# Mixer and FFN in one kernel: segment sums of ten tiles moved beside the FFN, its last products two tiles behind, and the first steps in another order

## The chip, the core and the metric

The kernel runs on one NeuronCore of a Trainium2 chip. The metric is the device time of one execution in microseconds (us). Three runs of the kernel before gave 1754.32 us in the median (1753.77 to 1755.31). Engines are named as in the profile: PE is TensorE (PEld its weight loads), DVE is VectorE, ACT is ScalarE, POOL is GpSimd, SP is SyncE, which issues most of the DMAs.

## What is computed

The input is `hidden_states`, 4 sequences of 256 tokens and 512 features, so 1024 tokens (T). It is normalised once (`xn`) and goes into two branches; the result is `x + s * g`.

```python
zxbcdt = xn @ in_proj_w.T            # gate 8192 | x 8192, B 1024, C 1024 | dt 128
xBC = silu(causal_conv4(xBC) + conv_b)
dt  = softplus(dt + dt_bias); Adt = -exp(A_log) * dt
L   = exp(segment_sum(Adt))          # decay from token j to token i, 0 for j > i
y   = ((C B^T) * L) @ (x * dt) + D * x         # per head; 128 heads of 64, 8 groups
s   = rmsnorm_per_group(y * silu(gate)) * norm_w @ out_proj_w.T
g   = silu((silu(xn @ gate_w.T) * (xn @ up_w.T)) @ down_w.T)   # FFN, 1792 wide, ternary weights
```

The reference works in chunks of 32 tokens; the kernel works with blocks of 128, two for each sequence, which gives the same sums. `segment_sum` of a row of `Adt` is, in the kernel, one scan along the free axis of a tile of 128 x 1024: `state = (state + m) * after`, where `after` is 1 above the diagonal of each block and 0 elsewhere. The row of a head is the same on all 128 partitions.

## The kernel before

**Two parts.** The first, `front` (from the start to 310.2 us in the profile), runs the normalisation, the FFN and, woven into it, `dt`, and for each of the 8 groups the tiles of B and C and their block products ("scores"). The second is a loop of 64 steps (L767), one for each tile of 128 channels of `x` (two heads) and of the gate.

**front.** The FFN has two halves of the tokens by 14 tiles of 128 of its width, so 28 tiles in sequence (L534). A tile makes `pg` and `pu` (16 products into two PSUM banks, L285), `sg = silu(pg) * pu` (ACT L539, DVE L548), splits it into a high and a low part `hh` (ACT L563) and `hl` (DVE L565), and adds 8 products of the tile before to four accumulators `pf` (`down`, L293). So the last products of a tile are made one tile behind. POOL casts the ternary weights (L225). `ffn_out` (L297) scales the finished accumulators, takes their SiLU and stores them.

Three times in each tile `next(pieces)` (L540, L551, L564) runs one turn of `all_pieces` (L481), so there are 84 turns. `bc_pieces(g)` (L413) begins at turn 11 + 8g and takes 14 turns: the products of B and C for a group, four sums of weights on DVE for the next group (`combine_to`), four additions (L434, L437, L440), three convolution taps for each of B and C (L181), two SiLUs and the score blocks (L460, L463). From turn 20 on `early_pieces` (L469) takes five turns for each of the 11 tiles 1 to 11: it loads the weights of that tile into `wq`, makes their four sums with `combine_to` into `sq`, and stores them in the DRAM tensor `early`.

**The sums of weights.** The products of a step are made with seven block products in place of eight (Strassen's form, in Winograd's variant), so each pair of weight tiles needs four sums or differences of 128 x 256 (L142 to L146).

**A step i.** On PE: seven products of two matmuls each (L173: `px`, `pq`, `px`, `pz`, `px`, `px`, `pq`) for gate and `x` of tile i; between them the transposes of tile i-1 (L625); then 48 small products `py` of tile i-1 (L666: for each sequence those with `v0`, then `v1`, then `v0t`). From step 10 on, 24 or 32 products `po` of the output projection of the group before come in between (L722). On ACT: copies of PSUM halves, the convolution's SiLU (L186), the exponentials of the scanned tiles `m` (L615), `y_begin` (L652), squares for the norm (L861, L864), the scaling of `wo` by the norm's weights (L856), the last tap (L177), the gate's SiLU (L899, L903). On DVE, steps 1 to 8: scan of `m` (L612), gating of tile i-2 (L673), second scan, `m * gm` and `mo * gm` for two heads (L618, L619), `xpad` add (L873), `v0`, `v0t` (L633), `v1` (L642), `gT` add (L889), three taps (L181). Up to LEAD = 9 the convolution's SiLU and both exponentials of a tile are issued in the step after it, later in its own step.

**Order.** Each engine works through its own list in the order in which the program issues instructions (`manual_schedule`); waits are made by semaphores. SP's list holds the DMAs of both parts in that order. `m` has five buffers, `mo` four, `w` two, `sq`/`sqacc` one.

For tiles up to EARLY = 11 the step loads the weights and their sums (L801 to L803, L918) in place of making them; from step 11 on `combine_w` makes them on DVE. The sums of the output weights of a group (`right_factors`, L708: four differences of 128 x 1024) are made at wn = 7 (two), on = 0 and on = 1, for the first group in steps 9, 9, 10 and 11. `wn`, `on` count the steps of a group from step 2.

Of the kernel before, what the change touches and what calls it, by code (L numbers as in the profile page):

```python
# [74 lines left out]
LEAD = 9  # L75
EARLY = 11
# [5 lines left out]
def mixer_ffn(ctx: ExitStack, tc: tile.TileContext, x, in_w, conv_w, conv_b, dt_bias, a_log, d_col,  # L82
# [44 lines left out]
    early = dram.tile([EARLY, P, 4, KT // 2, P], F32, name="early")  # L127
# [59 lines left out]


    def front(pre, one_of, fp, f2, hp, wq):
# [31 lines left out]
        def cast_ffn(n):  # L221
            ws = []
            for tag, wi in loads.pop(n):
                w = fp.tile([P, HID], F32R, name=tag, tag=tag)
                nc.gpsimd.tensor_copy(w, wi)  # L225
                ws.append(w)
            return ws
# [241 lines left out]
        def early_pieces():  # L469
            for n in range(EARLY):  # L470
                w = wq.tile([P, 2, KT, P], F32, name="wq")
                for m, i in enumerate((n + 1, CT + n + 1)):
                    nc.sync.dma_start(w[:, m], in_w[i])
                for _ in range(2):
                    yield
                s = wq.tile([P, 4, KT // 2, P], F32, name="sq")
                yield from combine_to(s[:, 0], s[:, 1], s[:, 2], s[:, 3], w)
                nc.sync.dma_start(early[n], s)
                yield

        def all_pieces():  # L481

            turn, chains = 0, [first_pieces()]
            later = []
            while chains or later or turn < 11 + 8 * G:
                if turn == 6:
                    later.append(dt_pieces())
                if turn >= 11 and (turn - 11) % 8 == 0 and (turn - 11) // 8 < G:
                    chains.insert(0, bc_pieces((turn - 11) // 8))
                if turn == 20:  # L490
                    later.append(early_pieces())
# [41 lines left out]
        last = None  # L533
        for n, (h, f) in enumerate(steps):  # L534
            if n + 2 < len(steps):
                load_ffn(n + 2)
            pg = project_exact(ws[0], xh, xl)
            sg = fp.tile([P, HALF], F32, name="sg")
            nc.scalar.activation(sg, pg, AF.Silu, scale=gs[:, f:f + 1])  # L539
            next(pieces, None)  # L540
            if f == 1 and h:
                ffn_out(h - 1, done, (1, 2))
# [9 lines left out]
            if f == 1 and h:  # L552
                ffn_out(h - 1, done, (3,))
            if last:
                down(*last)
                if f == 0:
                    done = last[0]
            if f == 0:
                pfs = [p.tile([P, HID], F32, name="pf", tag=tag)
                       for p, tag in ((ps_o, "o"), (ps_o, "o"), (ps_y, "y"), (ps_y, "y"))]  # L560
            hh = fp.tile([P, HALF], F32R, name="hh")
            hl = fp.tile([P, HALF], F32R, name="hl")
            nc.scalar.copy(hh, sg)  # L563
            next(pieces, None)  # L564
            nc.vector.tensor_tensor(hl, sg, hh.bitcast(F32), ALU.subtract)  # L565
            if f == 0 and h:
                ffn_out(h - 1, done, (0,))
            last = pfs, f, hh, hl, wd
        down(*last)
# [3 lines left out]
        return held["a"]  # L573

    with (tc.manual_schedule(), tc.tile_pool(name="pre", bufs=NT) as pre,
          tc.tile_pool(name="one_of", bufs=1) as one_of, tc.tile_pool(name="fp", bufs=3) as fp,
          tc.tile_pool(name="f2", bufs=2) as f2, tc.tile_pool(name="hp", bufs=1) as hp,
          tc.tile_pool(name="wq", bufs=1) as wq):
        a = front(pre, one_of, fp, f2, hp, wq)
# [15 lines left out]
    def load_rows(ct):  # L595
        ms = []
        for h in range(2):
            m = mp.tile([P, T], F32, name="m")
            nc.sync.dma_start(m, rows[2 * ct + h, 0:T].partition_broadcast(P))
            ms.append(m)  # L600
        return ms
# [8 lines left out]

    def decay_scan(m):
        nc.vector.tensor_tensor_scan(m, m, after, 0.0, ALU.add, ALU.mult)  # L612
# [43 lines left out]
    def y_products(ps, vs, ms, offs):  # L656
# [4 lines left out]
        for b in range(NB):  # L661
            py = ps[b // 2][:, b % 2, :]
            for q, v, stop in ((0, v0, True), (1, v1, False), (1, v0t, True)):
                for h, d in enumerate(halves):
                    m = off[h][:, b, :] if v is v0t else diag[h][:, b, q, :]
                    nc.tensor.matmul(py[d, q * P:(q + 1) * P], v[:, b, h, :], m,  # L666
                                     start=False, stop=stop, skip_group_check=True)
# [9 lines left out]
    def come(g, k):  # L677

        return k // 2 if g == G - 1 else max(k // 2, k - 2)
# [82 lines left out]
    with tc.manual_schedule():  # L762
# [3 lines left out]
        sqacc = rs = ya = outs = left = nxt = ob = sa = sb = sc = None  # L766
        for i in range(CT):  # L767
# [31 lines left out]
            if i + 1 <= EARLY:  # L799
                w = wp.tile([P, 2, KT, P], F32, name="w")  # L800
                nc.sync.dma_start(w[:, 0], in_w[i + 1])  # L801
                nc.sync.dma_start(w[:, 1, 0:2], early[i, :, 3])
                nc.sync.dma_start(w[:, 1, 2:4], in_w[CT + i + 1, :, 2:4])  # L803
            elif i + 1 < CT:
                w = load_w(i + 1, CT + i + 1)
# [22 lines left out]
            if here:  # L828
                product(pq, s1, t1, True)
                product(px, s2, t2, False)  # L830
                nc.scalar.copy(gT[:, HALF:], px)  # L831
                if lead:
                    decay_exp(ms[i - 1][1])
                if i:
                    decay_scan(ms[i][0])

                product(pz, a12, x21, False, (0,))
            if old:
# [5 lines left out]
                yps[i - 1] = y_begin(i - 1, xTs[i - 1])  # L844
            if here:
# [4 lines left out]
                nc.scalar.copy(xpad_h[1], by_batch(px))  # L850
            if og >= 0 and on == 0:
                sd = norm_sums(sqacc)
# [4 lines left out]
            if older:  # L857
                yf = yg.rearrange("p b l -> p (b l)")
                if (i - 2) % PER_G == 0:
                    sqacc = sqp.tile([P, T], F32, name="sqacc")  # L860
                    nc.scalar.activation(sqacc, yf, AF.Square)  # L861
                else:
                    sq = sqp.tile([P, T], F32, name="sq")
                    nc.scalar.activation(sq, yf, AF.Square)  # L864
# [4 lines left out]
            if i < CT + 1 and wg >= 0 and wn == PER_G - 1:  # L869
                rights[wg], toms[wg] = right_factors(wos[wg])  # L870
                toms[wg].pop(0)()
# [4 lines left out]
            for n, turn in ((wg, PER_G - 1), (og, 0), (og, 1)):  # L876
                if i < CT + 1 and n >= 0 and on == turn:
                    toms[n].pop(0)()
            if here:
                product(px, a22, t4, False)  # L880
                nc.scalar.copy(xpad_h[0], by_batch(px))
                if i == 0:
                    decay_scan(ms[i][0])
                    decay_scan(ms[i][1])
                product(pq, s4, x22, False)
            if old and og < 0:
                vs.append(values_1(i - 1, xTs[i - 1]))
# [5 lines left out]
            if old and og >= 0:  # L893
                vs.append(values_1(i - 1, xTs[i - 1]))
            if here:
# [8 lines left out]
            if old:  # L904
                y_products(yps[i - 1], vs, ms.pop(i - 1), offs.pop(i - 1))
# [5 lines left out]
            if here:  # L911
                conv_taps(i, xTs[i], xpad)
# [3 lines left out]
                if i + 1 <= EARLY:  # L916
                    s = scp.tile([P, 3, KT // 2, P], F32, name="s")
                    nc.sync.dma_start(s, early[i, :, 0:3])  # L918
                    a = factors(w, s)
# [4 lines left out]
                if i:  # L924
# [46 lines left out]
        y_products(py, vs, ms.pop(last), offs.pop(last))  # L971
# [110 lines left out]
```

## Time and profile before

| what | value |
|---|---|
| median of three runs | 1754.32 us |
| the profiled execution itself | 1755.07 us |
| its span, first to last instruction | 1753.4 us, so 1.7 us lie around it |
| PE busy | 1723.2 us (98%) |
| DVE busy | 1449.3 us (83%) |
| ACT busy | 1068.0 us (61%) |
| DMA | 342.16 MB, mean 195 GB/s |
| mean granted TensorE clock | 0.999 |

A line of the page's fifth part gives a group of instructions: line, engine, operation, output and inputs by name, shapes, count, then the busy time in us, the mean in ns of one, and the idle time of its engine just before it with what ended most of it. The view by windows gives the busy time of each engine in stretches of the span. The chain of waits follows the execution back from its last instruction, at each step to what released it. Busy PE is not PE at its peak, since ends of matmuls are modelled.

### The profile page before, as it was taken

How to read it: one execution, taken by the hardware profiler on the slowest of the kernel's cores; microseconds unless marked ns; L12 is line 12 of the kernel's file. 1: busy time of each engine (PE TensorE's matmuls, PEld its weight loads, DVE VectorE, ACT ScalarE, POOL GpSimd, SP SyncE). 2: the span in 40 equal slices, each digit the busy share in tenths (PEclk: the TensorE clock that was granted, in tenths of full speed). 3: DMA queues.
4: the chain of work that ended last, by engine and by line, in shares of the span. 5: the costliest groups of instructions: out<-in, count | busy, mean ns of one | idle time of the engine just before them, and what ended most of it. 6: DMA issues, size and time to landing. Idle time of an engine off the chain costs nothing.

```text
span 1753.4 us, 22592 instructions
## 1 busy us (share of the span) xinstructions
PE 1723.2 (98%) x8494; PEld 1106.2 (63%) x8494; DVE 1449.3 (83%) x1742; ACT 1068.0 (61%) x1418; POOL 196.8 (11%) x238
## 2 busy tenths in 40 slices
PE   9999999999999999999999999999999999999999
PEld 6566667445456666666666666666666666666677
DVE  5757666699988898889888888888888888888876
ACT  4544333577766666666666667666666666666640
POOL 3221121000000000111011101110111011101110
PEclk9999999999999999999999999999999999999999
DMA  6254553567767666776677667776777577757785
GB/s 228 79 185 154 213 180 109 188 217 227 214 205 208 201 199 193 210 202 185 199 213 200 193 185 214 199 206 179 214 199 216 166 214 201 215 165 214 212 231 172
DMA packets 164091, 342.16 MB, mean 195 GB/s; under 512 B 15376, under 2 KB 55952, under 8 KB 163984
## 3 DMA queue, kind: packets, MB, share of 16 engines
q1 hardware_dynamic: 141296, 287.78, 47.5%
q0 software_dynamic: 22688, 52.96, 17.0%
q8 instruction: 67, 1.10, 0.2%
q14 instruction: 40, 0.33, 0.1%
HBM read 236.08 MB, written 76.28 MB: 178 GB/s over the span
## 4 chain that ended last, share of the span: by engine, by line
PE 86%; DVE 10%; ACT 2%; issue 2%; DMA 1%; SPq 0%; ACTq 0%; DVEq 0%
PE px L173 24%; PE po L722 22%; PE pq L173 13%; PE py L666 9%; PE pz L173 6%; PE pp L285 4%; PE tp L625 3%; PE pf L293 2%; DVE m L612 2%; DVE xT L181 2%; PE pg L460 1%; DVE cT L181 1%; PE pv L684 1%; DVE m L618 1%; DMA m<-rows 1%
## 5 line engine op out<-in xcount | busy, mean ns | idle before, releaser
L612 DVE TENSOR_TENSOR_SCAN m<-m,after 128x1024 f32<-128x1024 f32 x128 | 292.1, 2283 | 0.4 <-DMA m<-rows 0.4
L173 PE MATMUL px<-xc,w 128*128 128x512 f32 x576 | 274.4, 599 | 6.2 <-ACT xpad L424 2.9
L181 DVE SCALAR_TENSOR_TENSOR xT<-xpad,cw,xT 128x1024 f32<-128x1024 f32 x192 | 246.2, 1282 | 4.6
L722 PE MATMUL po<-wo,ya 128*128 128x256 f32 x768 | 176.5, 379 | 0.0
L666 PE MATMUL py<-m,v 128*64 128x128 f32 x2048 | 160.6, 276 | 3.7 <-DVE v L642 3.7
L618 DVE TENSOR_TENSOR m<-m,gm 128x1024 f32<-128x1024 f32 x128 | 154.9, 1210 | 1.4 <-ACT m L615 1.4
L722 PEld LDWEIGHTS po<-wo,ya 128*128 128x128 f32 x768 | 141.5, 190 | 17.0 <-issue 0.2
L173 PEld LDWEIGHTS px<-xc,w 128*128 128x128 f32 x576 | 99.4, 191 | 81.2 <-issue 69.3
L908 POOL DMA_DIRECT2D sqacc<-sq x54 | 46.1, 853 | 898.5 <-ACT sq L864 852.6
L173 PE MATMUL pz<-xnT,w 128*128 128x512 f32 x288 | 146.1, 593 | 0.0
L173 PE MATMUL px<-xnT,w 128*128 128x512 f32 x288 | 141.9, 615 | 0.0
L173 PE MATMUL px<-xc,s 128*128 128x512 f32 x288 | 135.8, 594 | 4.9 <-ACT pz L821 2.1
L173 PE MATMUL pq<-xnT,s 128*128 128x512 f32 x288 | 136.8, 597 | 2.6 <-DVE xpad L873 1.7
L615 ACT ACTIVATE m<-m 128x1024 f32<-128x1024 f32 x128 | 135.3, 1058 | 0.7
L173 PE MATMUL pq<-xc,s 128*128 128x512 f32 x288 | 135.5, 593 | 0.3 <-DVE gT L889 0.3
L666 PEld LDWEIGHTS py<-m,v 128*64 128x64 f32 x2048 | 116.9, 137 | 25.7 <-issue 19.8
L625 PEld LDWEIGHTS tp<-ident,xT 128*128 128x128 f32 x512 | 67.7, 141 | 100.9 <-issue 86.6
L722 PE MATMUL po<-tw,sy 128*128 128x256 f32 x512 | 115.9, 379 | 0.0
L722 PEld LDWEIGHTS po<-tw,sy 128*128 128x128 f32 x512 | 97.2, 190 | 13.2
L831 ACT COPY gT<-px 128x512 f32<-128x512 f32 x64 | 37.4, 584 | 103.4 <-PE px L173 103.4
L173 PEld LDWEIGHTS px<-xc,s 128*128 128x128 f32 x288 | 54.2, 190 | 72.4 <-issue 65.3
L666 PE MATMUL py<-mo,v 128*64 128x128 f32 x1024 | 99.5, 273 | 0.0
(181 smaller groups left out, 3058.8 us busy)
## 6 DMA issues: line engine op xcount, KB each, us to landing
m<-rows SPq DMA_DIRECT2D x128, 512.0 KB, 6.4
w<-in_in_w SPq DMA_DIRECT2D x133, 256.0 KB, 6.9
mo<-rows SPq DMA_DIRECT2D x128, 256.0 KB, 7.2
gated<-yg SPq DMA_DIRECT2D x64, 512.0 KB, 8.3
ya<-gated SPq DMA_DIRECT2D x30, 1024.0 KB, 7.1
sqacc<-sq POOLq DMA_DIRECT2D x54, 512.0 KB, 5.9
wo<-in_out_w SPq DMA_DIRECT2D x64, 256.0 KB, 7.1
acc<-sa POOLq DMA_DIRECT2D x23, 512.0 KB, 5.8
```

What stands on the lines that cost most here:

```text
L173: nc.tensor.matmul(pp, a[:, k, :], b[:, k, :], start=start and k == 0, stop=k == KT // 2 - 1, skip_group_check=not start)
L181: nc.vector.scalar_tensor_tensor(xT, xpad[:, :, k:k + L], cw[:, i, k:k + 1], xT, ALU.mult, ALU.add)
L285: nc.tensor.matmul(pp, w[:, k * P:(k + 1) * P], part[:, k, :], start=(k == 0 and part is xh), stop=(k == KT - 1 and part is xl))
L293: nc.tensor.matmul(pf, part[:, i * P:(i + 1) * P], wd, start=(f == 0 and part is hh), stop=(f == FT - 1 and part is hl))
L612: nc.vector.tensor_tensor_scan(m, m, after, 0.0, ALU.add, ALU.mult)
L615: nc.scalar.activation(m, m, AF.Exp)
L618: nc.vector.tensor_mul(m, m, gm[:, 0:T])
L625: nc.tensor.transpose(tp[:, b, :], xT[:, b, c * P:(c + 1) * P], ident)
L666: nc.tensor.matmul(py[d, q * P:(q + 1) * P], v[:, b, h, :], m, start=False, stop=stop, skip_group_check=True)
L722: nc.tensor.matmul(po, a[:, k, :], b[:, k, :], start=start and k == 0, stop=k == HG - 1, skip_group_check=not start)
L831: nc.scalar.copy(gT[:, HALF:], px)
L908: nc.gpsimd.dma_start(sqacc, sq, accum_op=ALU.add)
```

## The change

It has these parts:

1. `early_pieces` no longer makes sums of weights. In 20 of the turns 23 to 80 (those with (t - 11) mod 8 of 2, 3 or 5, without 48) it scans the row tile of one of the 20 heads of tiles 0 to 9, and stores the result in `early`, now 20 tensors of 128 x 1024. The rows are loaded up to two ahead into three buffers.
2. The steps 0 to 9 load the scanned tiles (`load_rows` reads `early`) and scan nothing; they make the four sums of weights of the next tile themselves, two ahead of the first tap and two behind the last.
3. The FFN's last products run two tiles behind (`pending`); `wd` has four buffers, `wg` and `wu` two; `ffn_out` of the first half comes some turns later. The weights of tile 1 are loaded at the end of `front`.
4. In steps 0 to 9 (`fill`): the square comes ahead of the copy into `xpad` and `y_begin` behind it; the last tap and the first tap come ahead of `v1`, which comes ahead of the `gT` add; the products with `v1` come last for all sequences.
5. LEAD is 10, EARLY is 10. For the first group the output weights are loaded and scaled two for each step, and the first two differences of `right_factors` are made in steps 7 and 8.

```diff
-LEAD = 9
-EARLY = 11
+LEAD = 10
+EARLY = 10
...
-        def early_pieces():
-            for n in range(EARLY):
-                w = wq.tile([P, 2, KT, P], F32, name="wq")
-                for m, i in enumerate((n + 1, CT + n + 1)):
-                    nc.sync.dma_start(w[:, m], in_w[i])
-                for _ in range(2):
-                    yield
-                s = wq.tile([P, 4, KT // 2, P], F32, name="sq")
-                yield from combine_to(s[:, 0], s[:, 1], s[:, 2], s[:, 3], w)
-                nc.sync.dma_start(early[n], s)
+        def early_pieces(turn):
+            turns = [t for t in range(23, 81) if (t - 11) % 8 in (2, 3, 5) and t != 48]
+            ms, n = {}, 0
+            while n < 2 * EARLY:
+                if turn == turns[n]:
+                    m = ms.pop(n)
+                    decay_scan(m)
+                    nc.sync.dma_start(early[n], m)
+                    n += 1
+                for k in range(n, min(n + 2, 2 * EARLY)):
+                    if k not in ms and (turn not in turns or k == n):
+                        ms[k] = ep.tile([P, T], F32, name="em")
+                        nc.sync.dma_start(ms[k], rows[k, 0:T].partition_broadcast(P))
+                turn += 1
                 yield
...
-            if last:
-                down(*last)
+            if len(pending) == 2:
+                down_next()
...
-            nc.sync.dma_start(m, rows[2 * ct + h, 0:T].partition_broadcast(P))
+            nc.sync.dma_start(m, early[n] if ct < EARLY else rows[n, 0:T].partition_broadcast(P))
...
-                if i:
+                if i >= EARLY:
                     decay_scan(ms[i][0])
...
+            if older and fill:
+                square()
             if here:
                 product(px, s3, t3, False)
...
                 nc.scalar.copy(xpad_h[1], by_batch(px))
+            if old and fill:
+                yps[i - 1] = y_begin(i - 1, xTs[i - 1])
...
-            if i < CT + 1 and wg >= 0 and wn == PER_G - 1:
+            if wg >= 0 and wn == (PER_G - 1 if wg else PER_G - 3):
                 rights[wg], toms[wg] = right_factors(wos[wg])
...
-            if old and og < 0:
-                vs.append(values_1(i - 1, xTs[i - 1]))
+            if fill:
+                s = scp.tile([P, 3, KT // 2, P], F32, name="s")
+                sums = combine_to(s[:, 0], s[:, 1], s[:, 2], blocks(w)[2], w)
+                a = factors(w, s)
+                next(sums)
+                xTs[i] = xtp.tile([P, NB, L], F32, name="xT")
+                last_tap(i, xTs[i], xpad)
+                conv_taps(i, xTs[i], xpad, (0,))
+                if old:
+                    vs.append(values_1(i - 1, xTs[i - 1]))
...
-                conv_taps(i, xTs[i], xpad)
+                conv_taps(i, xTs[i], xpad, (1, 2) if fill else (0, 1, 2))
...
+                if fill:
+                    next(sums)
```

More of the change, by code (lines that the diff above doesn't have):

```diff
@@ L126, in mixer_ffn @@
     gated = dram.tile([CT, P, T], F32, name="gated")
-    early = dram.tile([EARLY, P, 4, KT // 2, P], F32, name="early")
+    early = dram.tile([2 * EARLY, P, T], F32, name="early")
     scores = dram.tile([G, P, ROW], F32, name="scores")
@@ L186, in conv_silu, with decay_scan, front @@
         nc.scalar.activation(xf, xf, AF.Silu, bias=cb[:, i:i + 1])
-    def front(pre, one_of, fp, f2, hp, wq):
+    def decay_scan(m):
+        nc.vector.tensor_tensor_scan(m, m, after, 0.0, ALU.add, ALU.mult)
+    def front(pre, one_of, fp, f2, hp, ep):
         ones = one_of.tile([P, P], F32, name="ones")
@@ L223, in cast_ffn @@
             for tag, wi in loads.pop(n):
-                w = fp.tile([P, HID], F32R, name=tag, tag=tag)
+                w = fp.tile([P, HID], F32R, name=tag, tag=tag, bufs=4 if tag == "wd" else 2)
                 nc.gpsimd.tensor_copy(w, wi)
@@ L489, in all_pieces @@
                     chains.insert(0, bc_pieces((turn - 11) // 8))
-                if turn == 20:
-                    later.append(early_pieces())
+                if turn == 21:
+                    later.append(early_pieces(turn))
                 if turn > 11 and (turn - 11) % 8 == 4 and len(chains) > 1:
@@ L532, in front, with down_next @@
             keep(t, tps[t])
-        last = None
+        pending = []
+        def down_next():
+            nonlocal pfs
+            f, hh, hl, wd = pending.pop(0)
+            if f == 0:
+                pfs = [p.tile([P, HID], F32, name="pf", tag=tag)
+                       for p, tag in ((ps_o, "o"), (ps_o, "o"), (ps_y, "y"), (ps_y, "y"))]
+            down(pfs, f, hh, hl, wd)
+        pfs = None
         for n, (h, f) in enumerate(steps):
@@ L539, in front @@
             nc.scalar.activation(sg, pg, AF.Silu, scale=gs[:, f:f + 1])
+            if f == 2 and h:
+                ffn_out(h - 1, pfs, (2, 3))
             next(pieces, None)
-            if f == 1 and h:
-                ffn_out(h - 1, done, (1, 2))
             pu, wd = project_exact(ws[1], xh, xl), ws[2]
@@ L551, in front @@
             next(pieces, None)
-            if f == 1 and h:
-                ffn_out(h - 1, done, (3,))
-            if last:
-                down(*last)
[L556 to L560, printed above, removed]
+            if len(pending) == 2:
+                down_next()
             hh = fp.tile([P, HALF], F32R, name="hh")
@@ L563, in front @@
             nc.scalar.copy(hh, sg)
+            if f == 1 and h:
+                ffn_out(h - 1, pfs, (0, 1))
             next(pieces, None)
             nc.vector.tensor_tensor(hl, sg, hh.bitcast(F32), ALU.subtract)
[L566 to L569, printed above, removed]
+            pending.append((f, hh, hl, wd))
+        w = load_w(1, CT + 1)
+        down_next()
+        down_next()
         ffn_out(1, pfs)
@@ L572, in front @@
             pass
-        return held["a"]
+        return held["a"], w
     with (tc.manual_schedule(), tc.tile_pool(name="pre", bufs=NT) as pre,
@@ L577, in mixer_ffn @@
           tc.tile_pool(name="f2", bufs=2) as f2, tc.tile_pool(name="hp", bufs=1) as hp,
-          tc.tile_pool(name="wq", bufs=1) as wq):
-        a = front(pre, one_of, fp, f2, hp, wq)
+          tc.tile_pool(name="ep", bufs=3) as ep):
+        a, w = front(pre, one_of, fp, f2, hp, ep)
     xtp = main.enter_context(tc.tile_pool(name="xtp", bufs=2, reuse_waits="tile"))
@@ L598, in load_rows @@
             m = mp.tile([P, T], F32, name="m")
-            nc.sync.dma_start(m, rows[2 * ct + h, 0:T].partition_broadcast(P))
+            n = 2 * ct + h
+            nc.sync.dma_start(m, early[n] if ct < EARLY else rows[n, 0:T].partition_broadcast(P))
             ms.append(m)
@@ L609, in load_off @@
         return offs
-    def decay_scan(m):
-        nc.vector.tensor_tensor_scan(m, m, after, 0.0, ALU.add, ALU.mult)
     def decay_exp(m):
@@ L654, in y_begin, with y_products @@
         return ps
-    def y_products(ps, vs, ms, offs):
+    def y_products(ps, vs, ms, offs, last_v1):
         v0, v0t, v1 = vs
@@ L660, in y_products @@
         halves = [slice(h * HD, (h + 1) * HD) for h in range(2)]
-        for b in range(NB):
-            py = ps[b // 2][:, b % 2, :]
[L663 to L667, printed above, removed]
+        parts = [(0, v0), (1, v1), (1, v0t)]
+        order = [(b, *p) for b in range(NB) for p in parts]
+        if last_v1:
+            order = [(b, *parts[n]) for ns in ((0, 2), (1,)) for b in range(NB) for n in ns]
+        for b, q, v in order:
+            py = ps[b // 2][:, b % 2, :]
+            for h, d in enumerate(halves):
+                m = off[h][:, b, :] if v is v0t else diag[h][:, b, q, :]
+                nc.tensor.matmul(py[d, q * P:(q + 1) * P], v[:, b, h, :], m, start=False,
+                                 stop=True, skip_group_check=True)
     def y_gate(ps, gT):
@@ L677, in come @@
     def come(g, k):
-        return k // 2 if g == G - 1 else max(k // 2, k - 2)
+        return k // 2 if g in (0, G - 1) else max(k // 2, k - 2)
     def norm_sums(sqacc, pool=ps_o, tag="o"):
@@ L765, in mixer_ffn @@
         xTs, gTs, yps, wos, rights, toms = {}, {}, {}, {}, {}, {}
-        sqacc = rs = ya = outs = left = nxt = ob = sa = sb = sc = None
+        sqacc = sq = rs = ya = outs = left = nxt = ob = sa = sb = sc = None
         for i in range(CT):
@@ L798, in mixer_ffn @@
                 ob = on // 2
[L799 to L804, printed above, removed]
+            fill = og < 0
+            if 0 < i < CT - 1:
                 w = load_w(i + 1, CT + i + 1)
@@ L843, in mixer_ffn, with square @@
                     nc.sync.dma_start(gm, scores[g])
-                yps[i - 1] = y_begin(i - 1, xTs[i - 1])
+                if not fill:
+                    yps[i - 1] = y_begin(i - 1, xTs[i - 1])
+            def square():
+                nonlocal sq, sqacc
+                yf = yg.rearrange("p b l -> p (b l)")
+                first = (i - 2) % PER_G == 0
+                sq = sqp.tile([P, T], F32, name="sqacc" if first else "sq")
+                nc.scalar.activation(sq, yf, AF.Square)
+                if first:
+                    sqacc = sq
+            if older and fill:
+                square()
             if here:
@@ L850, in mixer_ffn @@
                 nc.scalar.copy(xpad_h[1], by_batch(px))
+            if old and fill:
+                yps[i - 1] = y_begin(i - 1, xTs[i - 1])
             if og >= 0 and on == 0:
@@ L856, in mixer_ffn @@
                     nc.scalar.mul(wo, wo, nw[:, wg * PER_G + k:wg * PER_G + k + 1])
[L857 to L864, printed above, removed]
+            if older and not fill:
+                square()
             if og >= 0 and (here and on % 2 == 0 or i == CT - 1):
                 left_sums()
-            if i < CT + 1 and wg >= 0 and wn == PER_G - 1:
+            if wg >= 0 and wn == (PER_G - 1 if wg else PER_G - 3):
                 rights[wg], toms[wg] = right_factors(wos[wg])
@@ L875, in mixer_ffn @@
                 vs = values_0(i - 1, tp0)
-            for n, turn in ((wg, PER_G - 1), (og, 0), (og, 1)):
-                if i < CT + 1 and n >= 0 and on == turn:
+            for n, turn in ((wg, PER_G - 1 if wg else PER_G - 2), (og, 0), (og, 1)):
+                if n >= 0 and on == turn:
                     toms[n].pop(0)()
@@ L881, in mixer_ffn @@
                 nc.scalar.copy(xpad_h[0], by_batch(px))
-                if i == 0:
-                    decay_scan(ms[i][0])
-                    decay_scan(ms[i][1])
                 product(pq, s4, x22, False)
-            if old and og < 0:
-                vs.append(values_1(i - 1, xTs[i - 1]))
+            if fill:
[8 more added lines that the diff above has]
+                    vs.append(values_1(i - 1, xTs[i - 1]))
             if here:
@@ L892, in mixer_ffn @@
                     nc.vector.reciprocal(rs, sd)
-            if old and og >= 0:
+            if old and not fill:
                 vs.append(values_1(i - 1, xTs[i - 1]))
-            if here:
+            if here and not fill:
                 xTs[i] = xtp.tile([P, NB, L], F32, name="xT")
@@ L904, in mixer_ffn @@
             if old:
-                y_products(yps[i - 1], vs, ms.pop(i - 1), offs.pop(i - 1))
+                y_products(yps[i - 1], vs, ms.pop(i - 1), offs.pop(i - 1), fill)
             if older and (i - 2) % PER_G:
@@ L915, in mixer_ffn @@
                     conv_silu(i, xTs[i])
[L916 to L919, printed above, removed]
+                if fill:
+                    next(sums)
                 elif i + 1 < CT:
@@ L923, in mixer_ffn @@
                     ms[i + 1] = load_rows(i + 1)
-                if i:
+                if i >= EARLY:
                     decay_scan(ms[i][1])
@@ L970, in mixer_ffn @@
             next(outs)
-        y_products(py, vs, ms.pop(last), offs.pop(last))
+        y_products(py, vs, ms.pop(last), offs.pop(last), False)
         rights[G - 1], toms = right_factors(wos[G - 1])
```

## The prediction

> **What bounds the kernel now.** I read the page's chain first, then the windows cut at the steps (px of step 0 starts at 310.2 us, those of steps 1, 2, 3, 9, 10, 11, 12 at 322.4, 344.4, 361.6, 465.2, 484.1, 511.2, 532.2), then the chain inside an early step, then who made PE wait in `front`.
>
> ```profile
> PE 86%; DVE 10%; ACT 2%; issue 2%; DMA 1%; SPq 0%; ACTq 0%; DVEq 0%
> ```
>
> PE ends nearly everything; DVE ends a tenth, and it has a place:
>
> ```profile
> core 0: us, PE busy (x) PEld busy (x) DVE busy (x) ACT busy (x) POOL busy (x), PEclk, DMA share, GB/s
> 12.00:310.20 298.20, 287.81 (x1142) 195.75 (x1141) 191.00 (x262) 125.65 (x169) 65.20 (x83) 1.00 0.45 159
> 322.40:344.40 22.00, 18.45 (x86) 9.03 (x84) 16.89 (x17) 12.68 (x17) 0.00 (x0) 0.92 0.36 134
> 361.60:378.90 17.30, 16.65 (x87) 8.62 (x85) 15.92 (x17) 13.54 (x17) 0.89 (x1) 1.00 0.75 236
> 465.20:484.10 18.90, 16.64 (x86) 8.61 (x84) 18.26 (x19) 12.32 (x15) 0.85 (x1) 1.00 0.84 251
> 484.10:511.20 27.10, 25.00 (x135) 16.32 (x133) 24.37 (x26) 18.08 (x23) 0.00 (x0) 1.00 0.39 141
> 511.20:532.20 21.00, 21.00 (x110) 13.09 (x108) 17.50 (x20) 14.99 (x21) 0.84 (x1) 1.00 0.71 226
> ```
>
> Step 11 (the last row) has PE busy throughout; less its 24 `po` (5.18 us in the chain) a step needs 15.8 us of PE. Steps 2 to 8 take 17.26 each: 1.4 lost seven times. Step 1 loses 6.2, step 9 3.1, step 10 about 2.5 (27.1 less 15.8, 6.9 of 32 `po` and 1.9 of norm sums). The loop from step 11 on keeps its lists, so nothing is to be had there. Inside an early step:
>
> ```profile
> 355.87 1.98 PE pq L173 x4
> 357.86 0.45 PE tp L625 x4
> 358.33 0.69 DVE v L642
> 359.02 0.59 DVE gT L889
> ...
> 363.37 2.28 DVE m L612
> 365.65 1.18 DVE yg L673 x2
> 366.83 2.20 DVE m L612
> ...
> 372.49 0.61 DVE xpad L873
> 373.14 1.98 PE pq L173 x4
> ```
>
> The loop is DVE from `v1` (358.33) to the `xpad` add (373.10), 14.8 us without a gap, then `pq` and the transposes, 2.5 us: 17.26. In `front` the waits of PE are:
>
> ```profile
> PE px L173 <- ACT xpad L424: 2.9, 2, 1.6
> PE pf L293 <- DVE hl L565: 2.8, 2, 1.7
> PE px L173 <- ACT cpad L424: 2.0, 2, 1.1
> ```
>
> **Part 1, steps 2 to 8.** Two scans of 2.28 go (-4.56), four sums come; with nothing beside them one takes 0.42 (timeline, step 11), so +1.7. DVE falls from 15.9 to 13.0 and is no longer the loop; the question is which wait ends last. From the start T of px, with distances of the step at 344.37: ACT copies pz at T+2.1, then SiLU 1.15, table load 1.28, exponential 1.06, copies gT at T+6.0, so the third px product starts at T+6.6 as now (unhindered it would be T+6.3). The second exponential and the square run to T+8.4; the xpad copy follows the product at T+8.5, y_begin (1.23) ends at T+10.2. DVE makes the four `m * gm` products behind the first exponential, T+6.1 to 9.55, the xpad add to 10.15, v0 and v0t to 11.35, two sums to 12.2. PE starts the fourth px product at T+9.4 and `pq` at T+11.1: the add is ready. ACT copies the other half at T+11.3, makes the last tap T+11.9 to 13.1; first tap on DVE to T+14.35, v1 to T+15.05. PE has the transposes at T+12.8 and the 32 products that don't need v1 from T+13.3 to 15.15; v1 is there. Next px: T+16.1. Gain 1.15 x 7 = 8.1 us. In steps 3 to 6 two scalings of `wo` (1.24) sit ahead of the second copy: T+11.47, +0.15, covered. The differences of `right_factors` (1.1 each) in steps 7 and 8 cost up to 0.3 each.
>
> DMA: a step loads 0.9 MB of weights and sums now, 0.5 MB then; the scanned tile is 512 KB as the broadcast row is. Landing takes 4 to 5 us in these steps; the tightest user, the sums, comes 10 us after issue. Nothing.
>
> **Part 2, step 1.** Without two scans, the taps of tile 0 end 1.3 us earlier (two sums are put in). SiLU, table load, exponential, gT copy follow in line, so PE stands about 2.0 us at the third px product, not 2.55 after 0.5 at the transposes. Then the trace shows the clock halved for 3.4 us:
>
> ```profile
> 329.00:332.50 3.50, 0.64 (x4) 0.30 (x3) 2.12 (x2) 3.47 (x5) 0.00 (x0) 1.00 0.30 117
> 332.80:336.20 3.40, 3.40 (x5) 1.35 (x4) 2.67 (x4) 2.03 (x4) 0.00 (x0) 0.50 0.00 0
> ```
>
> [...] I take nothing, as stands of 1.7 us in `front` left the clock at 1.00. Step 1 then ends 30.65 after step 0 begins, not 34.15: -3.5.
>
> **Part 3, steps 9 and 10.** Step 9 loses its scan and both differences: 16.1 for 18.9, -2.8. Step 10 gets scans, late exponentials and the left sums (2.7) ahead of its xpad add: T+13.3, where `pq` could start at T+13.05 behind the norm sums; 25.2 for 27.1, -1.8. Its first scan needs a row issued in step 9 behind a 1 MB load that waits for a store; I reckon T+3 against T+4.3, so it holds with 1 us to spare.
>
> **Part 4, front.** DVE gets 20 x 2.28 = 45.7 and loses 44 sums, 21.4 (11 x (0.544 + 0.531 + 0.455 + 0.418)): 191 becomes 215 of 298 us. By place: class 5 scans come behind the add L440, where DVE waits 6.9 us in all for ACT's tap; class 3 lie between the score products (L463, 24.3 us of waiting); class 2 ahead of them. Replaying the groups at 130, 193 and 203 us, each scan lies in such a wait or makes a reader of PSUM at most 0.9 late with a bank to spare. At 139 and 231 it was the old sums between cT's taps that held the cpad copy (1.1 each): gone. Two tiles behind, `hl` is ready a tile early: -2.8. The wait of 1.6 at 177 stands behind ACT's `ffn_out`, which moves: -1.5. Queues: on SP the store of a scanned tile waits for DVE at most 4 us, ahead of ternary loads that have two tiles (21 us) in hand; POOL only casts, and `wd` no longer waits for PE (69.7 us of that).
>
> [...] The row: taps take 1374 ns here, 1284 in the steps, 7% more, so 20 x 0.15 = 3. [...] Bounds of `front`: -8 (all three waits and 1.3 for bT go), +3 (five scans half exposed, nothing gained). I take -6.3 and +1 for new small stands: -5.3.
>
> **Sum:** -8.1 - 3.5 - 2.8 - 1.8 - 5.3 = -21.5. The profiled execution would take 1755.1 - 21.5 = 1733.6; the median stood 0.8 under it: 1733 us.
>
> **Rivals.** (a) v1 stands behind the first tap, which waits for ACT: if ACT's line is 1.2 us longer than I reckon, the steps keep 17.26 and the rest remains: -21.5 + 8.1, 1741. For: v1 has 0.1 in hand. Against: ACT is busy 13.5 of 17.3. (b) The front gains nothing: 1738. For: DVE's waits there are in order, and one late reader delays the next. (c) Slower: the scans land on PE's path. The rest gains 16.2; each exposed scan costs up to 2.28, so from 7 exposed the gain is gone, and from 9 it is slower than this measurement can miss. With 12 (27.4): 1765. Against: 83 us of DVE left there, waits of 24.3 and 17.7 at the very places.
>
> **Chances.** Forecast 0.55, (a) 0.2, (b) 0.17, (c) 0.08. Under 0.2% (3.5 us) counts as no change, about what a measurement can tell. All but (c) are faster; of (c) a third falls in the middle: faster 0.92, same 0.03, slower 0.05. Range: from -27.5 (front -8, clock and step 10 better) to 1744, which takes in (a) and (b) with 3 us: 1727 to 1744.
>
> **What would show it.** Steps 2 to 8 at 16.1 with DVE near 13; no half clock in step 1; `hl` gone from PE's waits before 310; px of step 0 at 305; L189 in `front` without PE waiting for L434, L437, L567. Wrong: steps above 17, PE waiting on L654, or step 0 after 310.

## The result and the profile after

The median of four runs is 1744.17 us (1742.93 to 1744.66) against 1754.05 (1752.30 to 1755.31) for the kernel before: ratio 0.9943, 95% interval 0.9926 to 0.9961. It is faster, but by 10 us and not by 21. The profiled execution took 1743.98 us with a span of 1742.3. Its chain, by engine:

```profile
PE 89%; DVE 3%; ACT 3%; DMA 3%; issue 1%; SPq 1%; POOL 0%; ACTq 0%; DVEq 0%
```

DVE's share has gone from 10% to 3%; DMA has 3%, where it had 1%. The windows answer to those of before, cut at px of steps 0, then at step 1, step 3, steps 9, 10 and 11 (same columns):

```profile
12.00:313.50 301.50, 288.06 (x1147) 196.71 (x1148) 218.23 (x240) 126.70 (x170) 79.98 (x83) 1.00 0.56 191
326.70:344.50 17.80, 15.35 (x84) 8.05 (x82) 13.86 (x19) 12.08 (x16) 0.00 (x0) 1.00 0.20 62
360.80:377.10 16.30, 16.19 (x85) 8.66 (x85) 12.88 (x19) 13.45 (x18) 0.89 (x1) 1.00 0.77 227
458.90:475.10 16.20, 16.09 (x87) 8.67 (x85) 12.96 (x19) 12.40 (x16) 0.85 (x1) 1.00 0.79 243
475.10:500.10 25.00, 24.89 (x134) 16.37 (x132) 24.42 (x31) 17.93 (x24) 0.00 (x0) 1.00 0.35 124
500.10:521.10 21.00, 21.00 (x110) 13.13 (x108) 17.45 (x20) 14.99 (x21) 0.84 (x1) 1.00 0.69 226
```

The steps did what was wanted: 16.3 for 17.3, step 1 without half clock, step 10 in 25.0. The front did not: step 0 starts at 313.5, not at 310.2. For a point that is read alike in all runs I take ACT's copy of pz in steps 0, 2, 9 and 12:

| stretch | before | after | forecast | measured |
|---|---|---|---|---|
| start to copy of step 0 | 312.3 | 315.5 | -5.3 | +3.2 |
| steps 0 and 1 | 34.15 | 31.08 | -3.5 | -3.1 |
| seven steps from step 2 | 120.9 | 114.4 | -8.1 | -6.5 |
| steps 9 to 11 | 66.9 | 62.25 | -4.6 | -4.7 |
| from there to the end | 1219.13 | 1219.10 | 0 | 0 |

The sum is -11.1, the difference of the spans. The forecast was 10.4 us off, and 8.5 of them lie in the front. What PE waited for there (us in all, times, longest), in the kernel after:

```profile
PE px L173 <- ACT xpad L427: 5.7, 5, 1.7
PE pg L463 <- ACT bT L186: 3.4, 2, 3.1
PE tp L262 <- DVE xt L254: 1.9, 2, 1.1
PE px L173 <- ACT cpad L427: 1.8, 3, 1.4
```

The waits for hl are gone, as forecast, but xpad has gone from 2.9 to 5.7 and bT from 1.3 to 3.4; with the small ones the sum is 13.4 for 10.4. The chain behind one of the five waits for xpad:

```profile
228.16 0.83 SPq L133
...
229.04 7.49 DMA w<-in_in_w
...
236.56 0.44 DVE s L142
...
237.36 1.69 DVE bT L181
...
239.15 0.60 ACT xpad L427
...
239.79 1.98 PE px L173 x4
```

Columns are start, us, and what ran; read it from the bottom up. PE waits for ACT's copy into xpad; ACT waits for DVE's last tap of the group before, which still reads xpad; DVE had stood at the first of the sums of weights (L142) until the weights of the next group landed, 7.5 us after SP issued them. The chains of the other four, which end at 84.6, 147.3, 179.1 and 270.4 us, have the same links from the landing on. What held SP before it issued these weights stands in its list. First the kernel after, then the same group in the kernel before:

```profile
214.72 1.25 SPq L486 DMA_DIRECT2D em<-rows  x2
224.97 0.32 SPq L481 DMA_DIRECT2D early<-em  x1
...
228.16 2.59 SPq L133 DMA_DIRECT2D w<-in_in_w  x2
```

```profile
221.34 0.33 SPq L467 DMA_DIRECT2D scores<-sc  x1
221.76 2.64 SPq L133 DMA_DIRECT2D w<-in_in_w  x2
```

SP stands from 216 us until it can issue the store of a scanned tile at 224.97, then issues five other DMAs, and only then the weights, over 6 us later than in the kernel before. The two views that give the sizes are DVE's waits and SP's:

```profile
DVE s L142 <- DMA w<-in_in_w: 11.6, 5, 3.6
SPq L481 <- DVE em L189: 136.6, 20, 11.1
```

The first was 1.0 before. The second is the wait of SP's list for the 20 scans (the store of a scanned tile can't be issued before its scan has ended), up to 11.1 us at a time. SP stood for DVE in the kernel before too (94 us for the stores of the sums, up to 13.4 at a time), but there the weights came late only once: what counts is which loads stand behind the wait. For the stands at 179, 240 and 270 us the weights are issued 4 to 7 us later than in the kernel before. The other two have another start: at 84.6 SP had waited 28.8 us for `adt` (L346), as it did before, where PE stood 1.3 us at this place; at 147.3 the weights are issued no later, but land 6.4 us after their issue where it was 3.5.

### The profile page after: what moved, and what is told of

It reads as the page before. It is cut to its first block, busy times and chain, and to the rows that moved or that the text cites. A ratio compares the mean times of both kernels' runs of the same rounds, so it can differ in the third digit from the quotient of the medians.

```text
span 1742.3 us, 22580 instructions
## 1 busy us (share of the span) xinstructions
PE 1718.9 (99%) x8494; PEld 1108.2 (64%) x8494; DVE 1446.9 (83%) x1742; ACT 1068.7 (61%) x1418; POOL 211.7 (12%) x238
## 4 chain that ended last, share of the span: by engine, by line
PE 89%; DVE 3%; ACT 3%; DMA 3%; issue 1%; SPq 1%; POOL 0%; ACTq 0%; DVEq 0%
PE px L173 26%; PE po L737 22%; PE pq L173 13%; PE py L681 10%; PE pz L173 7%; PE tp L637 3%; PE pp L288 3%; DMA w<-in_in_w 2%; PE pf L296 2%; PE pg L463 1%; PE pv L699 1%; DVE bT L181 1%; ACT m L627 1%; ACT xT L186 1%; DVE cT L181 0%
## 5 line engine op out<-in xcount | busy, mean ns | idle before, releaser
L189 DVE TENSOR_TENSOR_SCAN m<-m,after 128x1024 f32<-128x1024 f32 x108 | 246.5, 2282 | 0.0
L173 PEld LDWEIGHTS pq<-xc,s 128*128 128x128 f32 x288 | 54.6, 190 | 69.9 <-issue 61.2
```

The source lines that it names most:

```text
L173: nc.tensor.matmul(pp, a[:, k, :], b[:, k, :], start=start and k == 0, stop=k == KT // 2 - 1, skip_group_check=not start)
```

## The experiments

Two theories at first. **A:** SP's list holds up the weights of the next group, and DVE and PE wait for their landing. **B:** the 46 us of scans on DVE delay the taps by themselves. A third, **C**, is about the other part: in the last group the work that goes over DVE and ACT to bT is longer than what PE has beside it, so that two tiles behind only moves PE's stand from hl to bT. In the kernel after, the chain that ends this stand of 3.1 us is:

```profile
286.68 0.73 DVE sg L567
287.41 1.42 DVE cT L181
...
295.26 1.40 DVE bT L181
...
296.69 1.16 ACT bT L186
...
297.88 1.16 PE pg L463 x8
```

In the table, the second column is the start of ACT's copy of pz in step 0, the third how much of it a halved TensorE clock took (half the length of the halved stretches, explained at the end), the fourth the mean of the seven steps from step 2. Medians belong to different chips, so the ratio to the kernel before on the same chip is what compares. The second and third columns are of one profiled execution each; about 1 us of a difference between two of them can come from the first 47 us, before any scan.

| run | copy of step 0 | of it half clock | step | median us | ratio, 95% interval |
|---|---|---|---|---|---|
| after | 315.5 | 0 | 16.34 | 1744.17 | 0.9943 [0.9926, 0.9961] |
| w_sooner | 308.1 | 0 | 16.34 | 1737.23 | 0.9900 [0.9885, 0.9915] |
| store_late | 313.6 | 3.4 | 16.34 | 1742.46 | 0.9931 [0.9916, 0.9946] |
| one_behind | 323.1 | 5.1 | 16.34 | 1748.88 | 0.9964 [0.9951, 0.9977] |
| before_two_behind | 313.4 | 1.7 | 17.27 | 1756.17 | 1.0001 [0.9993, 1.0009] |
| both | 309.8 | 1.7 | 16.34 | 1738.30 | 0.9898 [0.9884, 0.9913] |
| both_start | 311.7 | 3.4 | 16.34 | 1738.57 | 0.9903 [0.9888, 0.9917] |
| both_no_scan | 309.5 | 1.7 | 16.34 | 1737.86 | 0.9897 [0.9880, 0.9913] |
| old_order | 318.4 | 3.4 | 17.02 | 1753.28 | 0.9985 [0.9976, 0.9995] |
| v1_old | 316.4 | 1.7 | 17.02 | 1751.56 | 0.9983 [0.9974, 0.9993] |
| act_old | 318.4 | 3.4 | 16.29 | 1744.36 | 0.9942 [0.9927, 0.9957] |
| drain | 311.8 | 3.4 | 16.34 | 1740.41 | 0.9918 [0.9903, 0.9933] |
| drain_one | 308.6 | 0 | 16.34 | 1736.51 | 0.9892 [0.9877, 0.9907] |
| sooner_one_behind | 312.6 | 3.4 | 16.34 | 1741.24 | 0.9915 [0.9898, 0.9933] |
| best | 307.7 | 0 | 16.29 | 1736.03 | 0.9890 [0.9875, 0.9904] |

**w_sooner: the weights three turns sooner.**

```diff
-            w = load_w(2 * CT + G + g + 1, 2 * CT + g + 1) if g + 1 < G else load_w(0, CT)
+            if g == 0:
+                held["next"] = load_w(2 * CT + G + 1, 2 * CT + 1)
+            w = held.pop("next")
...
             nc.vector.tensor_add(cpad_h[1], cpad_h[1], by_batch(pq))
+            if g + 2 <= G:
+                held["next"] = (load_w(2 * CT + G + g + 2, 2 * CT + g + 2) if g + 2 < G
+                                else load_w(0, CT))
             yield
```

> The changed kernel with one edit: the weights of the next group's B and C are asked for three turns sooner (behind the s4 product of the group before), so that they stand ahead of the stores of scanned tiles in SP's list. Theory A (SP's list: the store of a scanned tile waits for DVE, the weights of the next group stand behind it, DVE waits for their landing and the taps and PE with it): DVE's wait for these weights falls from 11.6 us to 3 or less, PE's wait for the xpad copies in the front from 5.7 to about 2, step 0 starts at 309 to 310 instead of 313.5, time about 1740 (4 less). Theory B (the 46 us of scans themselves keep DVE from the taps): the wait for the weights goes, but the taps come no sooner; PE still waits 5 us or more for xpad, time within 1 us of 1744.

PE's waits in the front of this kernel:

```profile
PE pg L468 <- ACT bT L186: 3.3, 1, 3.3
...
PE px L173 <- ACT xpad L429: 0.8, 1, 0.8
```

DVE no longer waits for weights at all. Of the five stands for xpad only the first is left, at 0.8 us; A had asked for about 2 in all. Step 0 comes 7.4 us sooner, more than the 4 that A gave: 5.6 of that are stands, and 1.0 was there at 46 us already, from the run's start. SP still waits 132.3 us for the scans: the wait was harmless in itself, what stood behind it was not. A holds and B falls for the four stands that went.

**store_late: the store two turns behind its scan, four buffers.**

```diff
+                while done and turn >= done[0][0]:
+                    nc.sync.dma_start(early[done[0][1]], done[0][2])
+                    done.pop(0)
...
                     decay_scan(m)
-                    nc.sync.dma_start(early[n], m)
+                    done.append((turn + 2, n, m))
...
```

> The changed kernel with the store of a scanned tile issued two turns behind its scan (and a fourth buffer for these tiles, so that no load waits for it). Theory A: SP's wait for the scans falls from 137 us to under 40, the weights of the next group are issued 3 to 5 us sooner, DVE's wait for them falls from 11.6 to about 4, time about 1741. Theory B: SP waits less, the time stays within 1 us of 1744.

SP's wait for scans fell to 90.9 only, not under 40, but DVE's wait for weights to 0.9 and PE's for xpad to 1.4. Only the stand at 84 us is left of the five. The weights issued at 164.19 and 253.04 us still take 6.7 us to land, and PE does not stand for them: it was the late issue that cost, not the longer landing. Without the 3.4 of half clock its front would be 310.2. So the same cause, reached from the other side. Theory A's time was met within 1.5 us, the size of SP's wait was not.

**both and both_no_scan: is the rest the scans' time?** The scan of turn 72 goes to turn 80 (`t != 48` becomes `t not in (48, 72)`), on top of w_sooner; the second run leaves out the 20 scans, so the decay of tiles 0 to 9 is not summed there.

> The kernel with the weights asked for sooner, and the scan of turn 72 (the last group's, between the last cpad addition and the taps of cT) made in turn 80 instead. Theory: this scan runs 1.2 us past the arrival of pu, everything behind it on DVE down to bT's last tap is late by that, and PE waits 3.4 us for bT at 287: the wait becomes about 2.2, time about 1736, step 0 about 1.2 sooner. Rival: bT's taps are late for another reason (all of DVE's list of that tile is longer than PE's), the wait stays at 3 or more.

> The same as the run labelled both, but the 20 scans in the front are left out (the rows are stored as they were loaded, so the decay of tiles 0 to 9 is not summed; every DMA stays). If the scans lie hidden in DVE's waits once the weights come in time, the front is no more than 1 us shorter than with them. If they still cost PE, it is 3 us or more shorter, and the wait for bT falls below 1 us.

The wait for bT stayed at 3.0 with the scan moved, and at 3.1 with no scan at all:

```profile
PE pg L468 <- ACT bT L186: 3.1, 1, 3.1
```

Copies of step 0 at 309.8 and 309.5: 20 scans of 2.3 us cost PE 0.3 us. My theory for `both` was wrong, and B is out for the stand for bT too. That the scans lie hidden in the front, as the forecast had it, is shown for the kernel whose weights come in time; the changed kernel as it is was not run without them.

**before_two_behind and one_behind: the FFN's last products alone.** The first is the kernel before with part 3 of the change only (its loads of tile 1 left as they were), the second the changed kernel without it.

> The kernel before with this part of the change alone: last FFN products two tiles behind, wd with four buffers, wg and wu with two, first half's output later. By my forecast the two waits for hl go, step 0 starts at 307.4 instead of 310.2, time about 1751.3. By theory C the one at 290 goes over into the wait for bT at 295: 1 us or less is gained, about 1753.2.

> The changed kernel with the last FFN products one tile behind again, as in the kernel before (the buffers of the casts stay as changed). By my forecast the two waits for hl come back and cost 2.8: about 1747. By theory C (in the last group PE only meets the next thing that DVE is late with: the wait for hl of 1.8 at 290 became a longer wait for bT at 294) about half of it or less: the wait for bT shrinks by 1.8 where hl's comes back, time 1744 to 1745.5.

Alone it gains nothing: 1.0001 [0.9993, 1.0009]. PE's waits in that front, 12 to 312 us:

```profile
PE px L173 <- ACT cpad L424: 3.8, 3, 1.4
PE pg L460 <- ACT bT L186: 3.2, 2, 2.7
PE tp L259 <- DVE xt L251: 1.8, 2, 1.2
```

With 1.0 for xpad and 0.6 for the small ones the sum is 10.4, what it was with hl's 2.8 in it. The stand of hl at 73 (1.1) is one for cpad at 76 (1.4), that at 290 (1.7) one for bT at 293, whose stand grows from 0.8 to 2.7, and at the start (21 to 24 us) the products of the first tile, which had filled PE between two transposes, are missing (1.8 for 0.4). For the last group that is theory C. The wait of 1.6 at 177 us is gone as well, so the move of `ffn_out` did what the forecast said; it went into the same sum. In the changed kernel, though, part 3 was worth more than C gave it: one_behind took 1748.88 where C expected 1745.5 at most. Of the 7.6 us by which its front is longer, 5.1 went to the halved clock and 1.7 to stands: the wait for xpad is 8.1 with one of 3.8, and 1.9 came in for `ffn_out` (xt L304). That late weights met a PE with less in hand fits this, but no run separates it.

**sooner_one_behind: one tile behind with the weights in time.**

> The changed kernel with the weights asked for sooner and the last FFN products one tile behind again. My forecast said that two behind are worth 2.8 us (hl's waits). By theory C they are worth about 1 once the weights come in time: the two stands for hl (1.7 and 1.8) come back, those for bT and cpad shrink by about as much, time 1738 to 1739. If two behind are needed, 1740 or more.

The front without half clock is 309.2 against 308.1, so part 3 is worth 1.1 here, about what C gave. The stands do not account for it: they sum to 7.8 against 7.7, and where the rest lies is open. The two stands for hl are 0.8 and 2.2, not 1.7 and 1.8, and a third of 2.2, for `ffn_out` at 180 us, had not been expected. The time, 1741.24, is on the other side of what I set as the bound, because 3.4 of the profiled execution went to the clock (granted 0.998). The one run of the four with a granted clock of 1.000 took 1738.46, within C's 1738 to 1739. So C is right on the size and silent on the clock.

**drain and drain_one: fill the stand before bT.** In the last tile but one, `down_next()` is called twice, or once, ahead of the score products, on top of w_sooner.

> The kernel with the weights asked for sooner, and in the last FFN tile but one the last products of both waiting tiles made before the first score product, where PE stands 3.3 us for bT. Theory C (the last group's chain on DVE and ACT, from pu over cT's and bT's taps to bT's SiLU, is about 3 us longer than the work that PE has beside it; two tiles behind only moved the stand from hl to bT): 3.7 us of products fill the stand, step 0 starts 3 us sooner, time 1734 or a little below. Rival: the chain moves along, since hl or the accumulators come in the way, and the stand stays over 2 us.

> The kernel with the weights asked for sooner, and in the last FFN tile but one the last products of the older waiting tile alone made before the first score product; its hl is ready 3 us before. Theory C: these 1.85 us fill more than half of PE's stand of 3.3 us for bT, 1.4 to 1.5 are left, no half clock follows, step 0 starts 1.8 us sooner than with the weights alone; time 1735 to 1736. Rival: the chain to bT starts later by as much, and the stand stays at 3.

`drain` missed: the rival was right, PE then stood 3.6 us for the younger tile's hl, which DVE makes behind a tap and a scan. `drain_one` took the stand from 3.3 to 1.6, but 1.1 came back as a wait of the next products for sg, so only 0.6 was gained. The profile does not show it in the copy of step 0 (308.6 against 308.1), since this run was 1.0 later already at the first stand for cpad (it ends at 75.66 against 74.66). With more work put before bT's products, bT comes no sooner and PE stands behind it instead: the list of DVE is the limit there, not a lack of work for PE. C's first half is confirmed, its cure is not one.

**both_start: one behind for four tiles, then two.**

> The same as the run above with the first four FFN tiles one tile behind, as before, and two behind only from the fifth on. Theory: with two behind, PE has no last products to put between the first transposes and stands 1.1 to 1.3 us more at 21 to 23 us; that comes back, step 0 starts 1.1 us sooner. Rival: the wait comes from the landing of x and moves only; nothing is gained.

Nothing gained: xt's wait fell from 3.3 to 1.6, and 0.7 came back in a new wait for xpad at 54; 0.7 of its later step 0 was there before 21 us, and 1.7 is half clock. The rival's second half stands: nothing is gained. Whether the landing of x is the reason is open.

**old_order, v1_old, act_old: what shortened the steps.** The first puts all of part 4's order back, the second only v1, the taps and the order of the products, the third only ACT's square and y_begin.

> The changed kernel with the order of the steps 0 to 9 as it was (y_begin and then the square where they were, v1 ahead of the taps and of the gT addition, the products with v1 for each sequence in turn), while the scanned tiles still come from DRAM and the sums of weights are still made in the step. If taking two scans out of DVE's loop was what shortened the steps, steps 2 to 8 stay at 16.3 to 16.6 and the time rises by 2 us at most. If the order was needed, they go back towards 17.3: 1749 to 1751.

> The changed kernel with the other part of the order as it was: v1 behind pq and the products with v1 for each sequence in turn (PE then meets v1 0.5 us too early), the taps behind it. Steps 2 to 8 go to about 16.75, 3 us in seven steps, and PE waits 0.4 for v in each; time 1747 to 1748. If ACT's part carried it: 16.3 to 16.4.

> The changed kernel with ACT's part of the order alone as it was (y_begin ahead of the xpad copy, square behind the scaling of wo). If this part carried the shorter steps, steps 2 to 8 return to about 16.8. If the other part did (v1 and its products), they stay within 0.15 of 16.32, and the time within 1.5 us of 1744.

With v1 in its old place the step is 17.02, with or without ACT's part; with ACT's part alone undone it is 16.29, a little better than as changed. So `act_old` met its second branch, `old_order` fell into the branch "the order was needed", and `v1_old` went further than the 16.75 and 1747 to 1748 us that I had expected. Waits of PE from 345 to 500 us in v1_old; in the kernel after this view is empty:

```profile
PE py L681 <- DVE v L654: 3.3, 8, 0.4
PE px L173 <- ACT gT L842: 1.8, 9, 0.2
```

So, undone in this order, the scans that left DVE's loop (with the sums that came) gave 17.27 - 17.02 = 0.25 a step, 1.7 us in seven; v1's place, with the taps and the order of the products, gave 0.68, 4.8 us. Of the 0.68, 0.4 is PE's wait for v1 and 0.2 that for gT. What v1's place alone would give with the scans still in the step was not run, so the two can't be priced apart from each other. The chain of v1_old shows why the scans alone gave so little:

```profile
426.83 0.45 PE tp L637 x4
...
427.31 0.70 DVE v L654
...
428.05 2.62 PE py L681 x44
```

Even with DVE at 13 us of 17, PE meets v1 at once, since v1 needs the transposes that end just before; other products put between the two hide its 0.7.

**best:** w_sooner, drain_one and the old order of ACT together.

> The run labelled drain_one with ACT's part of the order of the steps as before the change (16.24 in place of 16.32 for a step in the run of that edit alone): 0.5 us less than drain_one, about 1735.

It is 1.1% under the kernel before and the fastest run, but its interval covers those of drain_one and w_sooner; the one edit that counts is w_sooner.

## Why the prediction was wrong

- **The failed step** is in part 4, the front: "on SP the store of a scanned tile waits for DVE at most 4 us, ahead of ternary loads that have two tiles (21 us) in hand". It waited up to 11.1, and what suffered behind it were not the ternary loads but the weights of the next group, which are asked for about two turns, 7 us, ahead of their use and took 5.3 to 7.5 us to land. I counted which queue the store is in, and not every load behind it with its slack. Price: the wait for xpad went up by 2.8 where I had it fall by 1.5, so 4.3 of the 8.5.
- **The second step that failed: "Two tiles behind, hl is ready a tile early: -2.8".** The waits went and the gain did not: before_two_behind sums to 10.4 like the kernel before. What is late next is bT in the last group, on the same chain of DVE, cpad at 75 us, and the transposes at the start. In the kernel after these cost 2.1, 1.4 and 1.5 more than before. My +1 for "new small stands" was the term that should have held them; it was 4 short.
- **The waits for cpad at 139 and 231** fell from 1.0 and 1.1 to 0.2 each, as forecast. **The wait at 177** was rightly put down to `ffn_out`: it is gone in before_two_behind and in w_sooner. In the kernel after a stand of 1.7 is back at the same place, now behind the weights' landing.
- **The scans are hidden** once the weights come in time: shown by both_no_scan. Rival (c) did not come. Rival (b), a front that gains nothing, came nearest; the front even lost 3.2, and the sign set for being wrong, step 0 after 310, is what came. That 3.2 lies close to the bound of +3 is luck: that bound was reckoned from exposed scans. The other bound is off in its sum, since the three waits and bT's 1.3 make 9.0, not 8.
- **Steps 2 to 8:** mechanism right, size 16.34 for 16.1. By the starts of the matmuls the third px product begins at T+6.6 as reckoned, but its first matmul takes 0.70 us where the others take 0.59, so the fourth begins at T+9.5 for T+9.4. Smaller lags behind it (`pq` at 11.2 for 11.1, the transposes at 12.9 for 12.8, the products with `v0` at 13.5 for 13.3) bring the next px to T+16.3. Step 7 takes 16.59, 0.3 more, for the differences, as forecast. Rival (a) did not come: no wait for v1 is left.
- **Steps 0 and 1:** -3.1 for -3.5. Step 1 did what was reckoned and a little more: the half clock (3.4 us at 0.50 before) is gone and PE stands 1.8 us for 2.0, but the stand hangs on another cause than the SiLU and the table load, since the chain shows the load `m<-early`, issued at 326.0, landing at 331.95. The missing 0.4 is a stand of 0.7 where step 1's first `pq` meets gT's addition of step 0; it was 0.3 before, and in w_sooner it is 0.3 again. **Steps 9 to 11** are right to 0.1 (step 10 was put at 25.2 for 27.1, which is -1.9 and not -1.8).

Put together: -21.5, +8.5 for the front, +1.6, +0.4 and -0.1 for the steps, is -11.1, the measured one. With the weights in time the same change gives 1737 us, inside the range, though its front then gains 4.2 and not 5.3.

## What to carry to other kernels

Before moving a store into an engine's DMA list, write down every load behind it with its slack in us: a store that waits for a busy engine delays the tightest of them, not the nearest (here it waited up to 11.1 us, and the weights of the next group were issued over 6 us later). A wait that goes is a gain only if the work after it does not hang on the same chain; follow that chain to the next thing PE needs. And where an engine can start only at the very end of its input and is waited for at once (v1 behind the transposes), taking other load off it helps little: 0.25 us a step here. Put other work between the two as well.

## What the runs showed of the hardware

**The cost in halved clock did not follow the length of a stand.** In the kernel before, the clock is halved once ahead of the program's end, for 3.413 us (332.79 to 336.20, granted 0.50). A `px` matmul there takes 1061 ns, where the median is 592. Lost clock is reckoned here as half the halved time, so 1.7 us for such a stretch. The clock's records of this trace change at 96, 97 and 512 times 3.413 us after the first full-speed entry (5.1 us), the one change of the kernel after at 507 times (first entry at 9.6 us). PE's matmul time, summed in windows of 3.413 us cut at these multiples, was 0.83 us in the one ahead of the half clock (329.39 to 332.79). Leaving out the end of the program, the least in any other full-speed window is 1.54 in the kernel before (from 486.4) and 1.71 in the kernel after (from 176.8), and the clock stayed full behind both. How long PE stands did not decide it: in the kernel before a stand of 2.4 us (to 332.40, for gT) is followed by this half clock, in w_sooner one of 3.3 by none, though PE had only 0.25 us of matmuls from 287.0 to 290.4. The windows of w_sooner, cut so that the stand lies over two of them (1.95 and 1.57 us of matmuls), then those of drain, where two windows at half begin within a stand of 3.6 us (it ends at 293.35):

```profile
285.30:288.70 3.40, 1.95 (x9) 1.29 (x7) 3.40 (x5) 0.91 (x2) 1.03 (x2) 1.00 0.79 295
288.70:292.10 3.40, 1.57 (x11) 1.48 (x12) 3.40 (x3) 1.73 (x3) 3.40 (x2) 1.00 0.00 0
292.10:295.50 3.40, 3.40 (x21) 2.94 (x20) 3.40 (x3) 0.00 (x0) 0.22 (x1) 1.00 0.38 154
```

```profile
288.50:291.90 3.40, 1.27 (x6) 0.73 (x4) 3.40 (x2) 2.18 (x3) 3.37 (x3) 1.00 0.01 4
291.90:295.30 3.40, 1.95 (x5) 1.56 (x6) 1.40 (x2) 0.00 (x0) 0.86 (x1) 0.50 0.38 154
295.30:298.70 3.40, 3.40 (x14) 3.01 (x13) 0.25 (x1) 0.00 (x0) 0.00 (x0) 0.50 0.00 0
```

In the profiled fronts of the table 0, 1.7, 3.4 or 5.1 us went to the halved clock. Runs of one kernel differ too: of 25 runs of the kernel before on one chip, those with a granted clock of 1.000 have a span of 1751.2 us in the mean, those with 0.999, 0.998 and 0.997 have 1753.2, 1754.6 and 1755.3. The forecast took nothing for the clock; that held in the kernel after (1.00 in the front and in step 1). How little work in a window is followed by half clock was not shown more closely than by these rows, whose matmul times have modelled ends.

**Beside the scans the casts of POOL take longer.** The 84 casts took 86.7 us in `both` and 73.8 in `both_no_scan`: 0.64 more for each scan, three quarters of a cast of 0.88. (They took 67.8 in the kernel before; what the other 6 are is open.) The scans themselves are hardly longer, 2300 ns in the front against 2282 in the steps; the taps are, 1429 and 1396 against 1282. The forecast reckoned 3 us for the 20 scans, from the taps; the runs show 13 us in all on POOL in `both` and 0.4 on the scans of the kernel after. What makes the casts longer was not shown. In the kernel after, PE's matmuls wait for no cast in the front, and its weight loads for 0.9 us in all.
